# A four-layer graph network on one core: 18 instead of 16 SBUF places for adjacency tiles in layers 0 and 1, and another order of steps in layer 3's loop

## The chip, the cores and the metric

The kernel runs on one core of one Trainium2 chip. The metric is the device time of one execution in microseconds (us), the median of several runs of the same kernel. Engines are named as the profile names them: PE is TensorE (matmuls; PEld its weight loads), DVE is VectorE, ACT is ScalarE, POOL is GpSimd, SP is SyncE, which here only issues DMAs.

## The reference

There are 3327 nodes with 64 features and one dense adjacency matrix `adj` (3327 x 3327 f32, nearly all zeros). Four layers follow one another, with a layernorm and a relu between them, and each reads the whole adjacency:

```python
# layer 0: two gated graph convolutions, each one product with adj
def _ggc(x, adj, W, wih, whh, bih, bhh):
    m = adj @ (x @ W)
    gi = m @ wih.T + bih
    gh = x @ whh.T + bhh
    ...
    r = sigmoid(i_r + h_r); z = sigmoid(i_z + h_z)
    n = tanh(i_n + r * h_n)
    return (1.0 - z) * n + z * x
h = relu(_ggc(x, adj, W1, ...)); relu(_ggc(h, adj, W2, ...))

# layer 1: hyperbolic graph convolution
support_t = mobius_matvec(adj, logmap0(x, c), c)
proj(expmap0(support_t, c), c)

# layer 2: last 100 neighbours, weighted by rank
mask = (adj != 0); rank = cumsum(mask, axis=1)
k = minimum(deg, 100.0)
pos = rank - (deg - k)
w = mask * where(pos > 0, 0.5 ** (k - pos), 0.0)
out = w @ support + bias

# layer 3: attention over pairs of nodes in the Poincare ball
adj_att = sigmoid(left + right.T) * adj
x_local = _logmap(x[:, None, :], x[None, :, :], C)
support_t = einsum('ij,ijd->id', adj_att, x_local)
_proj(_expmap(x, support_t, C), C)
```

## The kernel before

**Blocks, groups and tiles.** The nodes are padded to 26 blocks of 128. The target nodes lie in two groups: g0 with six pairs of blocks, g1 with seven. `gs_` and `gf` are the names of g0 and g1 where side work is written. An adjacency tile is one block of source nodes against one group of targets: (0,k) is 128 x 1536 f32, 768 KB; (1,k) is 128 x 1792 f32, 896 KB. [...]

**The stream of tiles.** Layers 0 to 2 and layer 3 read adjacency tiles in one fixed list of 260 uses. `Stream` keeps them in places ("slots") of SBUF, and loads a tile into a place when it isn't there. The list has these stretches:

| stretch | uses | what it computes |
|---|---|---|
| FIRST | 0 to 25 | first convolution of layer 0, target group 0 |
| SECOND | 26 to 63 | first convolution, group 1 (26 uses); among them, from the tenth, 12 uses of group 0 for the second convolution |
| THIRD | 64 to 103 | the rest of the second convolution |
| LAYER1 | 104 to 155 | layer 1 |
| layer 2 | 156 to 207 | 26 masks of group 1, then 26 of group 0 |
| layer 3 | 208 to 259 | 52 pieces of another width, one for each attention step |

`Stream.done`, called after each use, looks AHEAD 6 uses (10 after SECOND). For each tile there that is missing it evicts the place whose next use is latest, unless that comes sooner than the use it loads for, and issues the load (line 377) on SP's queue. SP does so in order: a load waits for its place to come free, and later loads wait behind it. The number of places is 16 in layers 0, 1 and the first half of layer 2, 7 in its second half, and 4 in layer 3; `Stream.limit` gives it, and a place above the limit of the stretch of its next use counts as free.

**Layers 0 and 1** are one loop: `use` takes the next tile and issues its matmuls `bank<-adj,m_a` or `m_b` (line 620), 1.29 us of PE for a tile of group 0 and 1.504 us for one of group 1. Everything else of these layers (gates, layernorms, the products with weights, the maps of layer 1) is written as generators, the side chains. `weave.tick()` after each use lets each running chain issue its next piece of work; `weave.until` runs a chain out where its result is needed. The side chains of a group's first and second part (`parts_of`) have their own arrays: `big` gives an array of 8 x 64 f32 a partition for each name and part in the pool `w01`, and `gates` has v and e there. `evicted` puts sums into the arrays `m_t0` and `m_t1` of the pool p0.

**Layer 2** makes a mask of each tile (line 1529, VectorE), counts it with matmuls (line 1560), makes weights (line 1572, ScalarE) and multiplies by them (line 1584).

**Layer 3** goes over pairs of blocks in 13 phases: four within group 1 (m = 0 to 3), six between the groups (m = 4 to 9), three within group 0 (m = 10 to 12). `BETWEEN` is 4, `WITHIN` is 10. A phase has two halves b = 0, 1. Its steps and their engines:

| step | engine, line | what |
|---|---|---|
| distances(m,b,i) | PE, 1190 | products of a chunk i of pairs into the one PSUM buffer `pair0` |
| gelus, square | ACT, 1200, 1210 | distances become factors; gelus empties `pair0` |
| tanh_d, tanh_t | ACT, 1223, 1246 | attention, direct and turned pairs |
| attention_d, attention_t | DVE, 1257 | times the adjacency piece; each takes one piece and calls `stream.done` |
| turned(m,k,u) | PE, 1281 | transposes the factors into the PSUM buffer `pair1` |
| factors_d, factors_t | DVE, 1272, 1291 | attention times factors, direct and turned |
| gather_d, gather_t, singles | PE, 1294 | sums over sources |
| end(m) | | drops the phase's arrays; for m = 9 it starts a side chain |

The order in which the steps are issued, and so the order within each engine's queue, is written out by hand in `ORDER3`: a prologue for phase 0, then a loop body that is gone through once for each m from 0 to 14. A word of it is a name, by how many phases the step is late, and the step's arguments: in pass m, `gather_d.2.1` issues gather_d of phase m-2, half 1, and `distances.-1.0.0` that of phase m+1. A step that was issued before, as by the prologue, is left out. `tick.1` always runs the side chains on, `tick.0` only while m is below 4. The side chains of layer 3 are `nodes3(gs_)` at its start, which must be through before phase 4; `finish(gf)` (lines 1372 to 1460), started by `end` of phase 9 in pass 11; and `finish(gs_)` after the loop.

Of the kernel before, what the change touches and what calls it, by code (L numbers as in the profile page):

```python
# [8 lines left out]
F32 = mybir.dt.float32  # L9
# [9 lines left out]
D = 64  # L19
P = 128  # L20
# [22 lines left out]

SLOTS3, SLOTS2, SLOTS01 = 4, 7, 16


AHEAD = (6, 10)
# [23 lines left out]
GROUPS = [Group(0, 6), Group(6, HB)]  # L73
# [91 lines left out]
def places3():  # L165

    r, o = {}, 0
    for m, half, t, w in pieces3():
        r[m, half, t] = (o, w)
        o += w  # L170
    return r, o
# [20 lines left out]
def order3(text):  # L192
# [9 lines left out]
    order3(t)  # L202
    for t in (
        """
        distances.0.0.0 gelus.0.0.0 tanh_t.0.0.0 tick.0 tanh_t.0.0.1 attention_t.0.0 distances.0.0.1
        tick.0 tanh_d.0.0 attention_d.0.0 tick.0 gelus.0.0.1 square.0.0 tick.0 distances.0.1.0 gelus.0.1.0
        tanh_t.0.1.0 tick.0 tanh_t.0.1.1 distances.0.1.1 gelus.0.1.1 tick.0 square.0.1
        turned.0.0.0 tick.0
        """,
        """  # L210
        gather_d.2.1 gelus.0.0.0 attention_t.1.0 distances.0.0.1 tanh_t.0.0.0 factors_t.1.0.0
        tick.0 singles.2.1 end.2 tick.1
        gelus.0.0.1 square.0.0 attention_d.1.0 turned.1.0.1 tick.0 gather_t.1.0.0 distances.0.1.0
        factors_t.1.0.1 factors_d.1.0 tick.1
        tanh_t.0.0.1 gelus.0.1.0 tick.0 tanh_d.0.0 turned.1.1.0 gather_t.1.0.1 gather_d.1.0 attention_t.1.1
        factors_t.1.1.0 tick.1
        distances.0.1.1 singles.1.0 gelus.0.1.1 tick.0 square.0.1 attention_d.1.1 turned.1.1.1
        gather_t.1.1.0 distances.-1.0.0 factors_t.1.1.1 tick.0 factors_d.1.1 tick.1
        turned.0.0.0 tanh_t.0.1.0 tick.0 tanh_d.0.1 tanh_t.0.1.1 gather_t.1.1.1 tick.1
        """,  # L220
    )
]
# [2 lines left out]
class Stream:  # L225
# [16 lines left out]

    def limit(self, t):
        part = sum(t >= s for s in self.starts)
        return (SLOTS01, SLOTS01, SLOTS2, SLOTS3)[part]

    def next_use(self, s, t):

# [44 lines left out]
def gnn_kernel(ctx: ExitStack, tc: tile.TileContext, t, out):  # L293
# [4 lines left out]
    def left(name, **kw):  # L298
        return tc.tile_pool(name=name, bufs=1, side="left", reuse_waits="tile", **kw)

    def right(name, **kw):
        return tc.tile_pool(name=name, bufs=1, side="right", reuse_waits="tile", **kw)
# [6 lines left out]
    p0 = ctx.enter_context(left("p0"))  # L309
    slots_a = ctx.enter_context(left("slots_a"))  # L310
    cc = ctx.enter_context(ExitStack())
    slots_c = cc.enter_context(left("slots_c"))
    c012 = ctx.enter_context(ExitStack())
    slots_b = c012.enter_context(right("slots_b"))
    nd = c012.enter_context(right("nd"))
    c01 = ctx.enter_context(ExitStack())
    w01 = c01.enter_context(right("w01"))
    ps = ctx.enter_context(tc.tile_pool(name="ps", bufs=1, space=PSUM))

# [26 lines left out]
    places, _ = places3()  # L346
# [17 lines left out]

    def load_tile(s, key):
        sum_edges(stream.slots[s][1])
        pool = slots_a if s < SLOTS3 else slots_b if s < SLOTS2 else slots_c
        a = pool.tile([P, WIDE], F32, name="adj", tag=f"adj{s}")
        if len(key) > 2:
            o, w = places[key]  # L370
            src = t["adj3"][:, o : o + w]
        else:
            g, k = key
            w = 2 * GROUPS[g].w
            src = t[f"adj{g}"][k * P : (k + 1) * P, :]
        a = a[:, :w]
        nc.sync.dma_start(a, src)
        loaded[0] += 1
        if loaded[0] in between:
            between[loaded[0]]()  # L380
        return a
# [3 lines left out]
    stream = Stream(load_tile)  # L385
# [68 lines left out]
    def small(g, name):  # L454

        tag = f"s_{name}" if g.part is None else f"s_{name}_{g.part}"
        return p0.tile([P, GROUPS[1].nb], F32, name=name, tag=tag)[:, : g.nb]

    def big(g, name):

        if g.part is None:
            a = p0.tile([P, GROUPS[1].nb, D], F32, name=name, tag="b_" + name)
        else:
            a = w01.tile([P, 8, D], F32, name=name, tag=f"b_{name}_{g.part}")
        return a[:, : g.nb, :]

    def flat(a):
# [229 lines left out]
    for i, (ca, cb) in enumerate(starts):  # L697
        g = Group(ca, cb, part=i % 2)
# [5 lines left out]
    def take_sums(g, acc):  # L704

        for q, (lo, hi) in enumerate(g.chunks):
            cs = slice(g.c0 * P + lo, g.c0 * P + hi)
            V.tensor_copy(mh0[:D, cs], acc[q][:D, : hi - lo])  # L708
            S.activation(hm1[D:, cs], acc[q][D:, : hi - lo], AF.Copy)  # L709

    def gates(g, layer):

        w_mh, w_hm, b, brz = ggc[layer]
        n, cs = g.w, g.cols
        ((p, _, _),) = pieces(1)
        ((p2, _, _),) = pieces(1)
        rz = [p[:, a * 512 : a * 512 + n] for a in range(2)]
        p_h, p_i = (p2[:, a * 512 : a * 512 + n] for a in range(2))

        def product(out, h, w, rs):  # L720
            T.matmul(  # L721
                out[D * (1 - h) : D * (2 - h), :],
                lhsT=w[rs, :],
                rhs=(mh0, hm1)[h][rs, cs],
                start=True,
                stop=True,
            )

        for a in range(2):
            for h in range(2):  # L730
                product(rz[a], h, (w_mh, w_hm)[h][:, a, :], slice(0, P))
        for out, o in ((p_h, 0), (p_i, 1)):
            for h in range(2):
                r = D * ((1 - h) ^ o)
                product(out, h, (w_mh, w_hm)[h][:, 2, :], slice(r, r + D))
        s = []
        for a in range(2):
            s.append(w01.tile([P, 512], F32, name=f"gate{a}", tag=f"gate{a}")[:, :n])
            S.activation(s[a], rz[a], AF.Sigmoid, bias=brz[:, a : a + 1])
        r, z = s  # L740
        v = w01.tile([P, 512], F32, name="v", tag="v")[:, :n]
        V.scalar_tensor_tensor(v, p_h, b[:, 1, 2:3], r, op0=OP.add, op1=OP.mult)
        V.tensor_add(v, v, p_i)
        S.activation(v, v, AF.Tanh, bias=b[:, 0, 2:3])

        e = w01.tile([P, 512], F32, name="e", tag="e")[:, :n]
        V.tensor_sub(e, h_t[:, cs], v)
        V.tensor_mul(e, e, z)
        V.tensor_add(e, e, v)
        V.tensor_scalar(h_t[:, cs], e, 0.0, None, op0=OP.max)  # L750
        if layer == 0:
            S.activation(mh0[D:, cs], e[D:], AF.Relu)
            S.activation(hm1[:D, cs], e[:D], AF.Relu)
        yield 5
# [72 lines left out]
    n = len(s_src) + len(f_src)  # L827
# [10 lines left out]
    n = len(LAYER1) - len(f_src)  # L838
# [88 lines left out]
    gen_f = weave.add(support(gf, acc_f))  # L927
    run(LAYER1[n:], {0: acc_s}, m_a, {}, begun=(0,), ends=(0,))
    c01.close()


    turn["banks"] = (0, 1)
# [570 lines left out]
    def early3():  # L1503

        for name, *args in (("tanh_t", 0, 0), ("tanh_t", 0, 1), ("tanh_d", 0)):
            made3.add((0, name, *args))
            yield from STEPS3[name](0, *args)


    with ExitStack() as c2:  # L1510
# [101 lines left out]
        for n in range(len(work)):  # L1612
            mask(n + 2)
            for part in range(2):
                count(n, part)
                flush(n, 2 if len(todo) > 2 * LAG + 2 else 1)
                todo.append((n, part))
                weave.tick()
            if gen_n or todo[0][0] < NB:
                continue  # L1620

            m_f = evicted(gf, acc2[1], b_l2)
            turn["banks"] = (2, 3)
            c2x.close()
            cc.close()
            stream.close(range(SLOTS2, SLOTS01))
            n3 = ctx.enter_context(left("n3"))
            h = n3.tile([P, NB, D], F32, name="h3")
            c3 = ctx.enter_context(ExitStack())
            n3f = c3.enter_context(left("n3f"))  # L1630
            xd = n3f.tile([P, NB, D], F32, name="xd")

            xs = n3f.tile([P, HN], F32, name="xs")
            xw = n3f.tile([P, HN], F32, name="xw")
            rows_j = n3f.tile([P, NP], BF16, name="rows_j")
            rows_i = n3f.tile([P, NP], BF16, name="rows_i")
            leftb = n3f.tile([P, NP], F32, name="leftb")
            p2c = n3f.tile([P, NB, 31 + ROWS], F32, name="p2c")
            x2, qs, pn, rpn, lefts, righth, B1, Bq2, alq = (
                n3.tile([P, NB], F32, name=n)  # L1640
                for n in "x2 qs pn rpn left righth B1 Bq2 alq".split()
            )
            least = n3.tile([P, 2], F32, name="least")

            packs = [n3f.tile([P, GROUPS[1].nb, P], BF16, name=f"pack{i}") for i in range(2)]
            for a in packs:
                G.memset(a, 0.0)
            G.memset(p2c, 0.0)
            onesl = n3f.tile([12, P], BF16, name="onesl")
            V.tensor_scalar(onesl, last[:12, :].to_broadcast([12, P]), 9.0, None, op0=OP.is_ge)  # L1650
            gen_n = weave.add(nodes3(gf, m_f))
            weave.add(early3(), 1, gen_n)
# [46 lines left out]
    with ExitStack() as cg:  # L1699
# [164 lines left out]
        for o, (g, half) in enumerate(segments):  # L1864
# [6 lines left out]
            for b0 in range(0, g.n, 4):  # L1871
                bs = own[b0 : b0 + 4]
                p = scratch3(b0 // 4)
# [92 lines left out]
            p = scratch3(0)  # L1966
# [101 lines left out]
```

## Time and profile before

| what | value |
|---|---|
| runs | 733.91, 732.25, 730.86 us; median 732.25 |
| the profiled execution's own time | 728.92 us |
| its span in the profile | 727.1 us |
| mean granted PE clock | 0.959 |
| busy: PE, DVE, ACT | 647.2, 463.7, 400.9 us |
| loads of adjacency tiles and pieces | 116 of 896 KB, 92 of 768 KB, 12 of 640 KB |
| use 63, the last of SECOND, on PE | 122.71 to 124.43 us |
| use 155, the last of LAYER1, starts | 292.71 us |
| layer 3's loop | about 430 to 707 us |

A row of the profile's windows gives the length of a stretch, then the busy time of PE, PEld, DVE, ACT and POOL in it with the number of instructions, the granted share of PE's clock, the mean busy share of the core's 16 DMA engines, and GB/s. The page's slice rows have 40 digits, each the busy share of 18.2 us in tenths (9 is 90% or more). The chain of waits follows the work that ended last back from its end; its rows give a start, a length and what the time went to. A row of the waits names the instruction that waited, and behind the arrow what it waited for, then the sum in us, the number of times and the longest.

### The profile page before, as it was taken

What the parts mean: (1) busy time and instruction counts of PE and PEld (TensorE: products, weight loads), DVE (VectorE), ACT (ScalarE), POOL (GpSimd) and SP (SyncE); (2) the same over time, 40 slices, a digit from 0 to 9 for tenths busy, and PEclk for the clock granted to TensorE, in tenths of its full rate; (3) what the DMA queues carried; (4) which work ended last, traced back from release to release, by engine and by line L of the source; (5) the groups of instructions that cost most, each with busy time, mean ns of one, the idle gap of its engine ahead of it and who ended that gap; (6) DMA issues with size and microseconds to landing.
All of it is one profiled execution on the core that took longest, in us unless ns stands there. A gap on an engine that the chain in (4) does not pass through costs nothing.

```text
span 727.1 us, 13405 instructions
## 1 busy us (share of the span) xinstructions
PE 647.2 (89%) x5648; PEld 358.8 (49%) x5648; DVE 463.7 (64%) x758; ACT 400.9 (55%) x577; POOL 6.5 (1%) x11
## 2 busy tenths in 40 slices
PE   3989998999979997889989985899999999998873
PEld 2433442343324332468856652456556666666552
DVE  4314774444778207676576464578888888877884
ACT  3203100302555013788887867688888888885912
POOL 0000000000000000000300000000000000000000
PEclk9999999999999999999999995699999999999995
DMA  8999997599979999999388750146566666553410
GB/s 339 414 415 410 383 357 290 182 405 418 415 270 372 417 415 418 416 368 356 103 290 268 297 159 17 37 138 190 193 199 204 203 204 204 188 175 94 146 49 26
DMA packets 33331, 189.90 MB, mean 261 GB/s; under 512 B 3696, under 2 KB 4848, under 8 KB 33264
## 3 DMA queue, kind: packets, MB, share of 16 engines
q1 hardware_dynamic: 33264, 188.97, 69.7%
q8 instruction: 46, 0.75, 0.4%
q14 instruction: 21, 0.17, 0.1%
HBM read 188.10 MB, written 0.85 MB: 260 GB/s over the span
## 4 chain that ended last, share of the span: by engine, by line
PE 60%; DMA 15%; DVE 13%; ACT 9%; issue 2%; SPq 0%; DVEq 0%; ACTq 0%
PE bank L620 18%; DMA adj<-in_adj 15%; PE bank L1294 13%; PE pair L1190 7%; PE pair L1560 6%; PE bank L1584 5%; PE pair L1281 4%; PE pair L721 2%; ACT tr L1246 2%; DVE dir L1272 2%; DVE dir L1257 1%; ACT w L1572 1%; ACT sq L1200 1%; ACT dir L1223 1%; PE bank L1382 1%
## 5 line engine op out<-in xcount | busy, mean ns | idle before, releaser
L620 PE MATMUL bank<-adj,m_a 128*64 128x384 f32 (+1 forms) x832 | 157.7, 520 | 11.7 <-DMA adj<-in_adj 10.8
L620 PEld LDWEIGHTS bank<-adj,m_a 128*64 128x64 f32 x832 | 56.1, 138 | 103.7 <-issue 65.7
L1572 ACT ACTIVATE w<-pair,ebias 128x896 uint16<-128x896 f32 (+1 forms) x101 | 93.9, 954 | 16.9 <-PE pair L1560 15.6
L620 PE MATMUL bank<-adj,m_b 128*64 128x384 f32 (+1 forms) x416 | 76.7, 515 | 1.4 <-ACT hm L709 1.4
L1529 DVE TENSOR_SCALAR mask<-adj 128x1792 bf16<-128x1792 f32 (+1 forms) x52 | 53.5, 1050 | 24.0 <-PE pair L1560 24.0
L1200 ACT ACTIVATE sq<-pair 128x1024 f32<-128x1024 f32 (+1 forms) x52 | 47.3, 910 | 38.0 <-PE pair L1190 38.0
L1246 ACT ACTIVATE tr<-leftb,righth 128x256 f32<-128x256 f32 x156 | 67.5, 495 | 0.0
L1291 DVE SCALAR_TENSOR_TENSOR tr<-pair,tr 128x1024 f32<-128x1024 f32 (+3 forms) x52 | 50.0, 961 | 26.1 <-PE pair L1281 23.5
L358 DVE SCALAR_TENSOR_TENSOR edges<-adj,edges 128x1792 bf16<-128x1792 f32 (+1 forms) x24 | 45.0, 1890 | 31.1 <-DMA adj<-in_adj 30.9
L1190 PE MATMUL pair<-xs 64*128 64x512 f32 (+3 forms) x120 | 58.0, 570 | 4.8 <-ACT sq L1200 4.7
L1190 PE MATMUL pair<-xs,xw 64*128 64x512 f32 (+3 forms) x120 | 58.0, 570 | 4.7 <-ACT sq L1200 4.7
L1584 PE MATMUL bank<-w,m_b 128*64 128x384 bf16 (+1 forms) x416 | 60.6, 341 | 0.0
L709 ACT ACTIVATE hm<-bank 64x384 f32<-64x384 f32 (+1 forms) x8 | 4.1, 513 | 90.9 <-DVE mh L708 90.8
L1281 PE MATMUL pair<-ident,sq 128*128 128x128 f32 x312 | 47.8, 290 | 7.2 <-DVE tr L1291 3.6
L1257 DVE SCALAR_TENSOR_TENSOR dir<-dir,adj 128x1792 f32<-128x1792 f32 x26 | 52.4, 2016 | 0.0
L1272 DVE SCALAR_TENSOR_TENSOR dir<-sq,dir 128x1792 f32<-128x1792 f32 x26 | 52.4, 2015 | 0.0
L620 PEld LDWEIGHTS bank<-adj,m_b 128*64 128x64 f32 x416 | 29.0, 137 | 45.6 <-issue 42.4
L1223 ACT ACTIVATE dir<-leftb,righth 128x1792 f32<-128x1792 f32 (+6 forms) x38 | 48.4, 1306 | 0.0
L1281 PEld LDWEIGHTS pair<-ident,sq 128*128 128x128 f32 x312 | 35.0, 146 | 26.8 <-issue 13.7
L1210 ACT ACTIVATE sq<-sq,hg 128x1792 f32<-128x1792 f32 x26 | 46.5, 1790 | 0.8
L1294 PE MATMUL bank<-tr,xd 128*64 128x128 f32 x624 | 46.7, 286 | 0.3 <-DVE tr L1291 0.3
L1294 PE MATMUL bank<-dir,xd 128*64 128x384 f32 (+3 forms) x264 | 44.0, 463 | 2.4 <-DVE dir L1272 2.3
(299 smaller groups left out, 998.3 us busy)
## 6 DMA issues: line engine op xcount, KB each, us to landing
adj<-in_adj SPq DMA_DIRECT2D x116, 896.0 KB, 6.9
adj<-in_adj SPq DMA_DIRECT2D x92, 768.0 KB, 9.1
adj<-in_adj SPq DMA_DIRECT2D x12, 640.0 KB, 4.0
xn<-in_x SPq DMA_DIRECT2D x3, 192.0 KB, 5.3
w_l<-in_w_l SPq DMA_DIRECT2D x1, 460.0 KB, 9.8
out<-h_n SPq DMA_DIRECT2D x2, 224.0 KB, 2.3
out<-h_n SPq DMA_DIRECT2D x2, 192.0 KB, 2.4
xn<-in_x SPq DMA_DIRECT2D x1, 256.0 KB, 6.9
```

The lines of the kernel that those rows point to most:

```text
L620: T.matmul(acc[q][h * D : (h + 1) * D, : hi - lo], lhsT=m[:, k, :], rhs=a[:, h * g.w + lo : h * g.w + hi], start=first, stop=last,)
L1190: T.matmul(p[:, o : o + n], lhsT=l, rhs=r, start=not rows, stop=rows)
L1200: S.activation(columns(sqs[m, b], PHASES[m].n)[:, :, lo * P : hi * P], p[:, :, : (hi - lo) * P], AF.Gelu, scale=-HA,)
L1223: S.activation(columns(dirs[m, b], ph.n)[:, :, first * P : first * P + n], left_of(ph.g)[:, :, o : o + n], AF.Tanh, bias=righth[:, 2 * c + ...
L1246: S.activation(a[:, e * 2 * P : (e + 1) * 2 * P].rearrange("p (b c) -> p b c", b=2), left_of(ph.s)[:, :, o : o + P], AF.Tanh, bias=righth[ ...
L1257: V.scalar_tensor_tensor(a[:, :w], a[:, :w], 1.0, stream.tile(stream.now), op0=OP.add, op1=OP.mult)
L1272: V.scalar_tensor_tensor(a, sqs[m, b][:, :n], HD, a, op0=OP.add, op1=OP.mult)
L1281: T.transpose(p[:, o : o + P], columns(sqs[m, b], PHASES[m].n)[:, k, i * P : (i + 1) * P], ident,)
L1294: T.matmul(out, lhsT=lhsT, rhs=rhs, start=False, stop=True, skip_group_check=True)
L1529: V.tensor_scalar(masks[n][:, :w], a, 0.0, None, op0=OP.not_equal)
L1572: S.activation(w, e, AF.Relu, bias=ebias)
L1584: T.matmul(acc2[i][q][h * D : (h + 1) * D, : hi - lo], lhsT=p[:, 2 * c + a, :], rhs=ws[n][:, h * g.w + lo : h * g.w + hi].bitcast(BF16), s ...
```

## The change

It has two parts.

Layers 0 and 1 have 18 places for tiles, layer 2's first half 16 as before: places 16 and 17 lie in a new pool `slots_d` that is closed with layer 1. The room comes from the side chains' arrays. `big` of a part becomes a slice of one array in p0 that both parts share (the second part begins at block 6), and v and e of `gates` lie in `m_t0` and `m_t1`. The instructions of the side chains stay the same.

Layer 3's steps stay the same too, but both texts of `ORDER3` are new. In the loop body, gather_d of the phase before goes from two passes late to one (`gather_d.1.1` for `gather_d.2.1`), and all its gathers stand at the end of the pass behind `turned.0.0.0`; attention_t.0.0 and gelus of the next phase (`gelus.-1.0.0`) stand a pass earlier; tanh_d's second half goes to the head of the next pass. The ticks are 7 of `tick.0` and 5 of `tick.1` for 6 and 5, two of the latter side by side; the prologue has 7 ticks as before.

In the changed kernel the line numbers of layers 0 to 2 are some 6 to 9 higher, those of layer 3's steps by 9 (1190 becomes 1199).

```diff
-SLOTS3, SLOTS2, SLOTS01 = 4, 7, 16
+SLOTS3, SLOTS2, SLOTS1, SLOTS01 = 4, 7, 16, 18
...
-        distances.0.0.0 gelus.0.0.0 tanh_t.0.0.0 tick.0 tanh_t.0.0.1 attention_t.0.0 distances.0.0.1
-        tick.0 tanh_d.0.0 attention_d.0.0 tick.0 gelus.0.0.1 square.0.0 tick.0 distances.0.1.0 gelus.0.1.0
-        tanh_t.0.1.0 tick.0 tanh_t.0.1.1 distances.0.1.1 gelus.0.1.1 tick.0 square.0.1
-        turned.0.0.0 tick.0
+        distances.0.0.0 gelus.0.0.0 distances.0.0.1 tanh_t.0.0.0 attention_t.0.0 tanh_t.0.1.0
+        tanh_t.0.0.1 tick.0 tick.1 tick.0 gelus.0.0.1 distances.0.1.0 square.0.0 gelus.0.1.0
+        attention_d.0.0 tanh_t.0.1.1 distances.0.1.1 tick.0 tick.0 gelus.0.1.1 tick.0 tick.0
+        tanh_d.0.0 square.0.1 turned.0.0.0
         """,
         """
-        gather_d.2.1 gelus.0.0.0 attention_t.1.0 distances.0.0.1 tanh_t.0.0.0 factors_t.1.0.0
-        tick.0 singles.2.1 end.2 tick.1
-        gelus.0.0.1 square.0.0 attention_d.1.0 turned.1.0.1 tick.0 gather_t.1.0.0 distances.0.1.0
-        factors_t.1.0.1 factors_d.1.0 tick.1
-        tanh_t.0.0.1 gelus.0.1.0 tick.0 tanh_d.0.0 turned.1.1.0 gather_t.1.0.1 gather_d.1.0 attention_t.1.1
-        factors_t.1.1.0 tick.1
-        distances.0.1.1 singles.1.0 gelus.0.1.1 tick.0 square.0.1 attention_d.1.1 turned.1.1.1
-        gather_t.1.1.0 distances.-1.0.0 factors_t.1.1.1 tick.0 factors_d.1.1 tick.1
-        turned.0.0.0 tanh_t.0.1.0 tick.0 tanh_d.0.1 tanh_t.0.1.1 gather_t.1.1.1 tick.1
+        tick.1 tanh_d.1.1 factors_t.1.0.0 tick.0 distances.0.0.1 attention_d.1.0 tick.1
+        turned.1.0.1 tanh_t.0.0.0 factors_d.1.0 singles.2.1 gelus.0.0.1 distances.0.1.0 end.2
+        tick.1 square.0.0 factors_t.1.0.1 gather_t.1.0.0 tick.0 turned.1.1.0 gelus.0.1.0
+        tanh_d.0.0 attention_t.1.1 factors_t.1.1.0 tick.1 tick.1 distances.0.1.1 singles.1.0
+        gelus.0.1.1 tick.0 tick.0 square.0.1 attention_d.1.1 tanh_t.0.0.1 tick.0 turned.1.1.1
+        tanh_t.0.1.0 tick.0 distances.-1.0.0 factors_t.1.1.1 factors_d.1.1 tick.0 gelus.-1.0.0
+        turned.0.0.0 gather_t.1.0.1 gather_t.1.1.0 attention_t.0.0 gather_d.1.0 tanh_t.0.1.1
+        gather_t.1.1.1 gather_d.1.1
...
     def limit(self, t):
         part = sum(t >= s for s in self.starts)
-        return (SLOTS01, SLOTS01, SLOTS2, SLOTS3)[part]
+        return (SLOTS01, SLOTS1, SLOTS2, SLOTS3)[part]
...
     c01 = ctx.enter_context(ExitStack())
+    slots_d = c01.enter_context(right("slots_d"))
     w01 = c01.enter_context(right("w01"))
...
-        pool = slots_a if s < SLOTS3 else slots_b if s < SLOTS2 else slots_c
+        limits = ((SLOTS3, slots_a), (SLOTS2, slots_b), (SLOTS1, slots_c), (SLOTS01, slots_d))
+        pool = next(p for most, p in limits if s < most)
...
+    bigs = {}
+
     def big(g, name):
 
         if g.part is None:
             a = p0.tile([P, GROUPS[1].nb, D], F32, name=name, tag="b_" + name)
         else:
-            a = w01.tile([P, 8, D], F32, name=name, tag=f"b_{name}_{g.part}")
+
+            if name not in bigs:
+                bigs[name] = p0.tile([P, GROUPS[1].nb, D], F32, name=name, tag="b_" + name)
+            a = bigs[name][:, 6 * g.part :, :]
         return a[:, : g.nb, :]
...
+    spares = [p0.tile([P, GROUPS[1].w], F32, name="m_t", tag=f"m_t{i}") for i in range(2)]
+
     def gates(g, layer):
...
-        v = w01.tile([P, 512], F32, name="v", tag="v")[:, :n]
+        v, e = (a[:, :n] for a in spares)
...
-        e = w01.tile([P, 512], F32, name="e", tag="e")[:, :n]
...
     c01.close()
+    stream.close(range(SLOTS1, SLOTS01))
...
-            stream.close(range(SLOTS2, SLOTS01))
+            stream.close(range(SLOTS2, SLOTS1))
```

## The prediction

> **What bounds the kernel now.** I read the page's engine line and slices first, then the chain of waits in order of time, then windows of the stretches that the change touches, then the waits of layer 3's end.
>
> ```profile
> span 727.1 us, 13405 instructions
> PE 647.2 (89%) x5648; PEld 358.8 (49%) x5648; DVE 463.7 (64%) x758; ACT 400.9 (55%) x577; POOL 6.5 (1%) x11
> ...
> PE   3989998999979997889989985899999999998873
> ...
> DMA  8999997599979999999388750146566666553410
> ...
> PE 60%; DMA 15%; DVE 13%; ACT 9%; issue 2%; SPq 0%; DVEq 0%; ACTq 0%
> ```
>
> TensorE is busy nearly everywhere, so only a stretch where its digit falls can shorten, unless its work shrinks; and this change leaves the work as it is. Such stretches are few: the start, about slices 15 to 17 (LAYER1), slice 24 (entry of layer 3), and the last four. DMA ends 15% of the chain. Where? These four waits in a row are the largest (start in us, length, what):
>
> ```profile
> 227.84 16.36 DMA adj<-in_adj
> 244.21 17.52 DMA adj<-in_adj
> 261.76 15.77 DMA adj<-in_adj
> 277.59 15.07 DMA adj<-in_adj
> ```
>
> The windows (length, then busy time of PE, PEld, DVE, ACT, POOL, granted clock, DMA share, GB/s) say the same:
>
> ```profile
> 16.00:62.00 46.00, 41.57 (x240) 17.08 (x240) 11.85 (x41) 5.83 (x12) 0.00 (x0) 1.00 1.02 415
> 84.00:116.00 32.00, 32.00 (x186) 13.11 (x184) 21.45 (x12) 0.00 (x0) 0.00 (x0) 1.00 0.97 365
> 125.00:196.00 71.00, 70.18 (x411) 27.50 (x411) 36.59 (x64) 18.29 (x34) 0.00 (x0) 1.00 0.86 341
> 228.00:295.00 67.00, 61.13 (x329) 21.96 (x326) 27.29 (x98) 14.35 (x25) 0.00 (x0) 1.00 1.02 417
> ```
>
> A DMA share of 1.0 with idle PE is a stretch bound by loads: 16 to 62 (FIRST, where every tile is new) and the end of LAYER1, where from 259.6 to 292.7 each use starts 0.04 us after its tile lands. SECOND's last four uses (118.3 to 122.7) are like that too. The other two windows have a full PE: a load saved there is worth nothing by itself. For layer 3:
>
> ```profile
> 430.60:450.00 19.40, 11.26 (x39) 4.59 (x38) 10.26 (x18) 13.64 (x18) 0.00 (x0) 0.61 0.27 82
> 450.00:470.00 20.00, 13.25 (x80) 8.17 (x81) 12.20 (x35) 10.57 (x17) 0.00 (x0) 0.61 0.03 4
> 470.00:490.00 20.00, 18.90 (x226) 12.01 (x226) 15.36 (x20) 17.63 (x25) 0.00 (x0) 1.00 0.48 153
> ...
> 550.00:590.00 40.00, 39.98 (x454) 25.00 (x454) 35.32 (x22) 35.34 (x51) 0.00 (x0) 1.00 0.61 202
> 590.00:630.00 40.00, 39.97 (x482) 25.27 (x482) 35.21 (x23) 35.30 (x52) 0.00 (x0) 1.00 0.62 200
> ...
> 670.00:690.00 20.00, 15.71 (x164) 9.56 (x162) 16.91 (x26) 19.88 (x38) 0.00 (x0) 0.91 0.43 124
> ```
>
> From 550 to 650 PE is never idle (0.05 us in 100): a phase takes 18.3 us, a half 9.15, which is the sum of PE's steps in a half: distances 1.28 + 1.02, singles 1.66, turned 0.80 + 1.02, gather_t 1.02 + 0.71, gather_d 1.65. VectorE and ScalarE are busy 0.88 of it. An order of steps can't shorten that. PE's idle time lies at the entry (14.9 us from 430.6 to 470), in the within phases (2.9 from 470 to 550) and in the tail (9.4 from 650 to 706.8). The waits of the tail (us in total, times, longest):
>
> ```profile
> ACT sq L1200 <- PE pair L1190: 6.0, 1, 6.0
> PE pair L1190 <- ACT sq L1200: 5.8, 3, 2.5
> DVE f_e L1405 <- PE bank L1382: 5.2, 1, 5.2
> DVE f_nn L1452 <- ACT f_nn L1445: 2.6, 1, 2.6
> ```
>
> These are finish(gf), woven into the last phases. Its VectorE step waits 5.2 us for a matmul of its own (L1382) that stands in PE's queue behind distances (L1190), which wait for gelus (L1200) to empty pair0. VectorE is idle 5.22 us there, 1.82 at 663 and 2.64 at 673: 9.7 in all; then it is full from 676 to 705.
>
> [...] the 5.2 us above is a whole VectorE queue behind one step. [...] 0.61 granted from 430 to 470 and 1.00 where PE is full[...]. [...] the trace moves 415 to 417, 2.19 us for 896 KB and 1.89 for 768.
>
> **Part 1: 18 places.** I followed the stream's rule (evict what is used latest, look AHEAD 6 or 10 uses) over all 260 uses. Layers 0 and 1 need 120 tile loads for 128, 101.6 MB for 108.7: 7.1 MB, 17 us at 415 GB/s. By stretch: FIRST 31 and 31, SECOND 23 and 21, THIRD 34 and 32, LAYER1 40 and 36. What each is worth:
> - FIRST: 0, no tile comes twice.
> - SECOND: tiles (0,10) and (0,11) stay. The last uses are then PE's: use 60 starts at 116.33, three more at 1.505 put use 63 at 120.85, not 122.71: **−1.9**.
> - THIRD: 0. PE is idle 0.8 us of 71; DMA runs further ahead but the entry of LAYER1 waits for a side chain.
> - LAYER1: (1,15) and (1,16) are not loaded again, 2 × 2.19 = 4.4; with two places more one load fits ahead of the entry of layer 1, 2.2 sooner. Its last tile lands 4.4 + 2.2 = 6.6 sooner, at 286 for 292.7. PE alone would be there at 283, so the loads still decide: **−6.5** (5.5 to 7.5).
> - Layer 2: its first half loads 23 for 21, its second 23 for 22, as the places are closed before it. Cost 0: every tile landed at least 8.2 us before its mask (L1529); the loads that come anew have 10 us. Without that cover each costs 2.2.
> - The arrays put inside others: the parts' big arrays become slices of one, the gates' v and e lie in m_t0 and m_t1. No instruction more or less; the side chains' waits on VectorE, ScalarE and PE are the same in the two builds. Cost 0; layer 2's masks that lie over the new places start after use 154, no later than now.
>
> Sum **−8.4** (6 to 10).
>
> **Part 2: the loop of layer 3.** The same instructions, in another order. Every queue is concerned: on SP, the loads follow attention_t.0.0, which comes a pass sooner, so its piece's successor is asked for sooner; pieces have about 0.6 of the DMA, so 0 for that.
> - Steady phases, 550 to 650: 0, if PE stays full. What covers PE changes: see the slower rival.
> - Within phases: 2.9 us of PE idle, mostly L1190 waiting for L1200 (2.0). gelus.0.0.0 now stands at the end of the pass before, right after its distances, before the tick: **−2**.
> - Tail: the 5.22 goes down to about 1, since gelus come ahead of the tick and pair0 is free when finish(gf)'s matmul is queued; two ticks side by side hand VectorE the next step without a phase's step in between. The 2.64 (ScalarE's root behind a table load, 1.28) stays, of the 1.82 some. 9.7 to about 5, and as VectorE is full afterwards this passes to the end: **−4.5**. What is late next: VectorE itself, factors_d and attention at 2.02 each; the last 20.5 us, finish(gs), are as before.
> - Entry, 430.6 to 470: 12 ticks a pass for 11, as many in the prologue, distances.0.0.1 earlier. PE and ScalarE are both waiting there for nodes3(gs), a chain. No row shows the new order: bounded by −3 and +3, I take 0.
>
> Sum **−6.5**, from −11 to +4.
>
> **The number.** −8.4 − 6.5 = −14.9 on the profiled execution's 728.9 (span 727.1 + 1.8): 714.0. The median of the runs is 3.3 above that execution, 732.25, so **717.3**.
>
> **Rivals.**
> - The loop gives nothing, or costs a little (wait moves from L1405 to another step of the chain, the tail stays at 9.7 idle): 732.25 − 8.4 = 723.9, with +3 at the entry 727. For: ScalarE and VectorE at 0.88 leave little room. Against: the tail's wait has one nameable cause.
> - The loads saved don't pay: PE or the side chain support(gf), which ends near 284, is right behind, or the DMA falls idle elsewhere. Then −1 to −3 for part 1, and 722 to 725. For: 17 us of DMA give only 8.4 already. Against: DMA share 1.02 for 67 us.
> - **Slower**: pair0 is one buffer. distances.0.1.0 now comes straight after gelus.0.0.1; before, turned (1.02) and gather_t (1.02) lay between on PE. Now PE has turned 1.02 and singles 1.66 between the two distances, 2.7 us, while ScalarE must do tanh_t (four at 0.495, 2.0) and gelus (0.8), 2.8, and may still have tanh_d (1.78) before them. If PE stalls there in each half, some 20 halves pay: from 0.42 us a half the 8.4 are eaten, from 0.6 the kernel is over 0.5% slower, at 0.8 it is 16 − 8.4 = +7.6, **740**. Against: ScalarE has 1.2 us spare in each half, so it can be early.
> - The change doesn't do what it says: the slices serialise the two parts' side chains, and layer 1's entry slips. The build has the same waits, so I give it 1 in 100, in the slower case.
>
> **How the numbers follow.** Both parts pay, 712 to 721: 0.50. Loop for nothing or a small loss, 721 to 728: 0.23. Loads for little: 0.09. Ends even: 0.09. Slower: 0.09. A measurement of this kernel tells about 0.5% from no change, 3.7 us, so faster means under 728.6: 0.50 + 0.23 + 0.09 = 0.82 (a few of these cases end above, a few even ones below). Same 0.09, slower 0.09. The range, 707 to 729, leaves out the slower case, half of the even one and a gain beyond −25 (0.05); the likeliest case's own is 712 to 721.
>
> **What would show it.** Right: the page's adj issues fall from 220 (116 + 92 + 12) to 215; use 63 starts 1.9 us sooner, the last use of LAYER1 8.4; windows of the middle phases still 18.3 us a phase with PE full; the wait of L1405 below 2 us. Wrong: PE idle before L1190 (there L1199) in every half; mask waits on DMA in layer 2; an unchanged idle sum of VectorE in the tail.

## The result and the profile after

The changed kernel is faster: 711.72 us median (708.52 to 713.05, 4 runs) beside 732.03 us of the kernel before (730.86 to 733.91), a ratio of 0.971 (95% interval 0.967 to 0.976). The profiled execution took 713.05 us with a span of 711.2, which is 15.9 less than the span before. The medians are 20.3 apart, so both profiles together understate the gain by some 4 us; what follows accounts for the 15.9.

The page's head, the slices of PE and DMA, the chain by engine, and the loads of tiles:

```profile
span 711.2 us, 13400 instructions
...
PE 640.8 (90%) x5648; PEld 362.6 (51%) x5648; DVE 463.2 (65%) x758; ACT 401.5 (56%) x577; POOL 5.9 (1%) x11
...
PE   3988999999979998889998994699999999999692
...
DMA  8999996599959999978687942046666666654400
...
PE 67%; DMA 13%; DVE 9%; ACT 8%; issue 2%; SPq 1%; DVEq 0%; ACTq 0%
...
adj<-in_adj SPq DMA_DIRECT2D x110, 896.0 KB, 5.8
adj<-in_adj SPq DMA_DIRECT2D x93, 768.0 KB, 8.2
```

There are 215 loads (110 + 93 + 12), as forecast. PE's busy time fell by 6.4 us for the same 5648 matmuls, which the forecast had excluded. Waits for DMA at the end of LAYER1 in the chain (start, length):

```profile
237.83 16.91 DMA adj<-in_adj
254.76 16.52 DMA adj<-in_adj
271.36 15.06 DMA adj<-in_adj
```

Three rows where there were four, but still there: LAYER1 ends on its loads. The windows of layer 3 (length, busy time of PE, PEld, DVE, ACT, POOL, granted clock, DMA share, GB/s):

```profile
426.00:446.00 20.00, 9.29 (x50) 4.79 (x46) 14.25 (x28) 14.69 (x20) 0.00 (x0) 0.79 0.25 79
446.00:466.00 20.00, 14.98 (x84) 9.61 (x84) 8.73 (x25) 11.71 (x17) 0.00 (x0) 0.61 0.12 34
466.00:486.00 20.00, 19.54 (x250) 12.81 (x252) 17.49 (x22) 17.39 (x25) 0.00 (x0) 1.00 0.50 158
...
538.00:578.00 40.00, 40.00 (x470) 26.24 (x470) 35.93 (x23) 36.33 (x54) 0.00 (x0) 1.00 0.64 209
578.00:618.00 40.00, 40.00 (x458) 25.27 (x456) 35.95 (x24) 36.32 (x52) 0.00 (x0) 1.00 0.62 201
...
654.00:674.00 20.00, 14.06 (x155) 8.35 (x152) 17.88 (x38) 18.36 (x34) 0.00 (x0) 0.98 0.52 159
```

PE is full in the middle in both kernels, yet a phase takes 17.92 us where it took 18.30. The waits of the tail, from 630 to 691 us (total, times, longest):

```profile
DVE tr L1300 <- PE pair L1290: 5.0, 3, 1.9
ACT sq L1209 <- PE pair L1199: 4.5, 3, 2.5
...
PE pair L1290 <- ACT sq L1219: 2.8, 1, 2.8
DVE f_e L1414 <- PE bank L1391: 2.2, 1, 2.2
...
PE pair L1199 <- ACT sq L1209: 1.6, 1, 1.6
```

finish(gf)'s wait for its own matmul fell from 5.2 to 2.2 us, and its wait for ScalarE's root (2.6) is gone. VectorE's waits for turned (L1290) have grown to 5.0 us in three pieces; in the kernel before, from 645 to 707 us, they were

```profile
DVE tr L1291 <- PE pair L1281: 2.1, 2, 1.8
```

With landmarks that exist in both traces, the 15.9 us can be split. A landmark is the start of an instruction; fd(m,b) is factors_d of phase m, half b. Intervals in us:

| stretch | before | after | difference | forecast |
|---|---|---|---|---|
| start to use 63, last of SECOND | 122.7 | 120.7 | −2.0 | −1.9 |
| to use 155, last of LAYER1 | 170.0 | 165.7 | −4.3 | −6.5 |
| to the last product of layer 2 | 137.6 | 139.8 | +2.2 | 0 |
| to fd(0,1): entry of layer 3 | 46.3 | 44.2 | −2.1 | 0 |
| to fd(4,1): within phases | 73.1 | 68.6 | −4.5 | −2 |
| to fd(9,1): middle phases | 91.5 | 89.6 | −1.9 | 0 |
| to fd(12,1): tail | 61.9 | 59.3 | −2.6 | −4.5 |
| to the end | 24.0 | 23.3 | −0.7 | 0 |

The sum was forecast within 1 us (−14.9 for −15.9), out of terms that are wrong on both sides: that it came so near is luck. The experiments go after these terms.

### The profile page after: what moved, and what is told of

It is laid out like the page before. It is cut to its first block, busy times and chain, and to the rows that moved or that the text cites. A ratio compares the mean times of both kernels' runs of the same rounds, so it can differ in the third digit from the quotient of the medians.

```text
span 711.2 us, 13400 instructions
## 1 busy us (share of the span) xinstructions
PE 640.8 (90%) x5648; PEld 362.6 (51%) x5648; DVE 463.2 (65%) x758; ACT 401.5 (56%) x577; POOL 5.9 (1%) x11
## 4 chain that ended last, share of the span: by engine, by line
PE 67%; DMA 13%; DVE 9%; ACT 8%; issue 2%; SPq 1%; DVEq 0%; ACTq 0%
PE bank L626 21%; PE bank L1303 15%; DMA adj<-in_adj 12%; PE pair L1199 7%; PE pair L1569 6%; PE pair L1290 6%; PE bank L1593 5%; PE pair L730 2%; ACT w L1581 1%; DVE dir L1266 1%; DVE mask L1538 1%; PE bank L1391 1%; PE pair L531 1%; DVE dir L1281 1%; ACT sq L1219 1%
## 5 line engine op out<-in xcount | busy, mean ns | idle before, releaser
L1199 PE MATMUL pair<-xs,xw 64*128 64x512 f32 (+3 forms) x120 | 56.3, 555 | 5.4 <-ACT sq L1209 5.4
L1199 PE MATMUL pair<-xs 64*128 64x512 f32 (+3 forms) x120 | 56.3, 555 | 1.2 <-ACT sq L1209 1.2
L1290 PE MATMUL pair<-ident,sq 128*128 128x128 f32 x312 | 47.7, 290 | 10.7 <-ACT sq L1219 9.1
L1290 PEld LDWEIGHTS pair<-ident,sq 128*128 128x128 f32 x312 | 34.7, 145 | 29.3 <-ACT sq L1219 9.5
L1266 DVE SCALAR_TENSOR_TENSOR tr<-tr,adj 128x1280 f32<-128x1280 f32 (+2 forms) x26 | 45.5, 1750 | 1.6 <-ACT tr L1255 1.6
L1303 PE MATMUL bank<-dir,p2c 128*32 128x256 f32 (+1 forms) x440 | 45.3, 350 | 0.0
```

The source lines that it names most:

```text
L1199: T.matmul(p[:, o : o + n], lhsT=l, rhs=r, start=not rows, stop=rows)
L1266: V.scalar_tensor_tensor(a[:, :w], a[:, :w], 1.0, stream.tile(stream.now), op0=OP.add, op1=OP.mult)
L1290: T.transpose(p[:, o : o + P], columns(sqs[m, b], PHASES[m].n)[:, k, i * P : (i + 1) * P], ident,)
L1303: T.matmul(out, lhsT=lhsT, rhs=rhs, start=False, stop=True, skip_group_check=True)
```

## Experiments

Ratios are to the kernel before, with their 95% intervals; kernels without a ratio were run once, and are read by the intervals of the table. Two of these hardly depend on the run: 68.58 to 68.60 within phases and 89.63 or 89.64 in the middle, wherever nothing there was changed. The entry and the tail do depend on it, and so does the time that PE spends there at half its clock (granted 0.50): the same tail takes 61.9 us in the kernel before, 6.8 of them at half clock, and 65.1 in layout_only below, 13.7 of them at half clock.

### The two parts alone, and the shared memory alone

places_only is the changed kernel with the old texts of `ORDER3`; loop_only is the kernel before with the new ones; layout_only is places_only with

```diff
-SLOTS3, SLOTS2, SLOTS1, SLOTS01 = 4, 7, 16, 18
+SLOTS3, SLOTS2, SLOTS1, SLOTS01 = 4, 7, 16, 16
```

> 18 places in layers 0 and 1, layer 3's order as in the kernel before. Theory: the two parts add up, and this one brings what the traces show up to the last use of LAYER1: use 63 starts 2.0 us sooner, use 155 6.3 us sooner, layer 3's loop as long as before (430 to 707), so 6 us less, ratio about 0.991, 215 loads. Rival: the gain is lost again behind, in layer 2 or at the entry of layer 3, which waits for chains of its own: less than 3 us, ratio above 0.996. Second rival: the order of the loop hides part of the places' gain, then this run shows more than 8 us.

> 16 places, layer 3's loop in the new order. Theory: 12 us less, ratio about 0.983, made of 2 at the entry, 3 to 4 in the within phases, 2 in the middle phases (17.92 us a phase for 18.30), 3 to 4 in the tail; use 155 starts at 292.7 as before. Rival: the sum was owed to the earlier start of layer 3 [...], then 5 to 8 us.

> The arrays lie within others' memory as in the changed kernel, but layers 0 and 1 have 16 places, and layer 3's order is that of before: what the sharing of memory costs by itself. Theory: nothing, within 1 us of before, use 155 at 292.7. Rival: the parts' side chains wait for one another, and a stretch of layers 0 and 1 is 1 to 4 us longer, at most at the entry of layer 1 (use 104 later than 205.8).

places_only: 724.64 us, ratio 0.992 (0.990 to 0.995). loop_only: 718.82, ratio 0.984 (0.980 to 0.987). Their product is 0.976, beside 0.971 and 0.974 (0.971 to 0.978) for both together in two comparisons: the parts add up. In us, places_only is 6.3 faster than the kernel before and loop_only 12.1, where the forecast had 8.4 and 6.5: the loop brought nearly twice its share, the places less than theirs. layout_only: ratio 1.0001 (0.9986 to 1.0015): putting arrays inside others costs nothing that its 20 runs show.

In the one trace of layout_only use 155 started at 294.2, later than in the two others with 16 places (292.7 and 293.2), but 0.7 to 0.9 us of that stand already at use 63, which the traces with 18 places also have spread over 1.4 us (120.6 to 122.0; in places_only 122.0, so 0.7 sooner than before and not 2.0). With 18 places and the stream unchanged the eight traces at hand have use 155 from 284.7 to 287.2, 286.2 in the mean, so the places bring 7.1 us there on average, 2.0 of them by use 63, and the 6.3 of the first pair of traces is on the low side.

### The changed kernel again: what layer 2 lost

> The changed kernel once more, for its trace. Theory: the 2.1 us that its first trace lost in layer 2 (the lead fell from 6.3 to 4.1 us at 315) were a window of 3.4 us in which PE had half its clock after a pause, and such windows fall by chance: in this trace the lead at the end of layer 2 is 6 us or the window lies elsewhere, and the time goes with the number of such windows, some 1.7 us each at most. Rival: the loss is of the changed load plan, and stands in the same place with PE at full clock.

It took 712.00 us. Its layer 2 took 138.0 us, not 139.8, so the loss isn't part of the load plan. The windows of the first trace after, and of the same work before, show what it was:

```profile
314.00:318.00 4.00, 3.15 (x18) 1.90 (x19) 3.17 (x4) 2.70 (x3) 0.00 (x0) 0.61 0.56 182
```

```profile
318.00:322.00 4.00, 2.67 (x28) 1.83 (x29) 2.40 (x5) 3.83 (x6) 0.00 (x0) 1.00 0.90 360
```

In the upper row (after) PE is busy 3.15 us of 4 with 18 matmuls, in the lower (before) 2.67 us with 28: the granted clock is at half (0.50) for 3.4 us, from 314.9, and the lead over the kernel before falls from 5.9 to 4.2 us across it. This half-clock window follows pauses of PE of 1.0 and 1.1 us; the kernel before has the same two pauses there, and a clock of 1.00 behind them. What makes such a window isn't shown. Counted over the traces of the study, layer 2 takes 136.6 and 136.9 us without such a window (layout_only, ticks_apart), 137.5 to 138.4 with one (seven traces; ahead_at_entry below, whose first mask waits, is left out), 138.7 to 139.8 with two (four traces). After had two, before one.

### The places: 17, and a longer look ahead

places_17 has 17 for 18 in the first line above. ahead_at_entry is the changed kernel with

```diff
         most = AHEAD[self.now >= len(FIRST + SECOND)]
+        if 96 <= self.now <= 112:
+            most = 14
```

and ahead_16 has `102 <= self.now <= 120` and 16.

> The changed kernel with 17 places in place of 18. By the stream's rule layers 0 and 1 load 124 tiles (120 with 18, 128 with 16), and LAYER1 38 (36, 40). Theory: the gain of LAYER1 goes with its loads, one place is worth half: use 155 starts 2 to 3 us later than with 18, at 289 to 290, and use 63 within 0.5 us of it. Rival: the second place brings nothing more, since DMA falls idle at the entry of layer 1 for as long as a load is saved: 286 to 287.

> The changed kernel, but the stream looks 14 uses ahead from use 96 to 112, not 10. Theory: in the changed kernel DMA falls idle for 13 us around the entry of layer 1 (202 to 241 us) since all of the next 10 tiles are there; four more uses let three or so loads of LAYER1 go in that gap, so that the last tile lands 3 to 5 us sooner and use 155 starts at 282 to 284 for 286.5; layers 2 and 3 as they are: 3 to 4 us less than the changed kernel, ratio to before about 0.969. Rival: places, not the look ahead, hold the loads back, or the side chain support(gf) ends last: less than 1 us.

> The changed kernel, but the stream looks 16 uses ahead from use 102 to 120, not 10. In the run with 14 (96 to 112) use 155 started 3.4 to 4.1 us sooner than in the changed kernel, and most of it was lost as layer 2's first mask waited 2.9 us for tile (1,24), which that plan had evicted and loaded last. This plan keeps (1,24) to (1,21) in places that layer 2 can use. Theory: use 155 starts at 282 to 284, the first masks don't wait for DMA, and the lead of 3 to 4 us lasts to the end: ratio to before 0.967 to 0.970. Rival: another wait takes its place at the start of layer 2 (the side chain support(gf), or the masks' memory over places 16 and 17), and less than 1.5 us of it is left.

With 17 places use 155 started at 290.3: somewhat under half of the gain of 7.1, about as the loads of LAYER1 go (38, between 36 and 40). Its use 63 was at 122.1, 1.4 later than in the trace after, where at most 0.5 had been expected.

Why did the places bring 4 us in LAYER1 (5.1 in the mean of the traces), and not 6.5? The stream's rule, followed over the uses, asks for the same ten tiles of LAYER1 ahead of use 104 in both kernels; what the places save are two later loads, (1,15) and (1,16), the 4.4 us of the forecast. The other 2.2 were to come from one more load ahead of the entry, but a look of ten uses ahead doesn't ask for one.

In the trace after, all ten have landed at 202.54, before use 104 starts (203.40); in the kernel before three of them land after it (205.75). Then the stream is silent until 204.95: all of the next ten tiles are in their places while the entry of layer 1 waits for a side chain. The windows of that stretch, after and before:

```profile
202.00:241.00 39.00, 36.96 (x214) 14.74 (x214) 31.79 (x144) 16.33 (x31) 0.00 (x0) 0.95 0.79 294
```

```profile
202.00:241.00 39.00, 35.26 (x206) 13.63 (x204) 32.55 (x142) 18.23 (x33) 0.00 (x0) 0.96 0.83 328
```

In the upper row the DMA moves 294 GB/s, where from 16 to 62 us in the kernel before, at a share of 1.02, it moves 415; no packet at all is under way in 5.3 of these 39 us. Counted by landings, with 2.19 and 1.89 us for a tile of 896 and 768 KB, more is lost: 13.0 us in six pieces from 202 to 241 in the kernel after, 8.9 from 202 to 244 in the one before. So much of what fewer loads had freed was idled away before LAYER1's last loads began.

ahead_at_entry fills part of that (7.0 us are lost from 200 to 241): use 155 started at 283.1, 3.4 us sooner than in the first trace after and 4.1 than in the second. But the kernel gained nothing (711.47, ratio 0.973, 0.968 to 0.978). The mask's tile in its trace (from 278 to 292 us, the start of layer 2; what VectorE idled for before masks, and how long):

```profile
  DMA adj<-in_adj: 2.9, 1
```

The first mask's tile (1,24) had been in a place that layer 2 doesn't have; it was loaded once more, behind LAYER1's last tile, and landed at 285.24; the mask starts at 285.36. Of a lead of 4.1 us over the trace of after_again 1.0 was left at the first count. ahead_16 keeps that tile (2.1 us are lost): use 155 started at 283.0, no mask waits for DMA, and the time is 707.69 us (705.89 to 708.26), ratio 0.969 (0.966 to 0.972). That is the version which beats both kernels; its interval overlaps that of the changed kernel, but its four runs lie below all eight of that kernel (708.52 to 713.05), and its trace shows 3 to 4 us at the end of LAYER1 that last.

### The loop: prologue, gelus, ticks, gathers, end

Five runs of the changed kernel with one thing, or one group of words, put back. Once each, they took 714.7 (old_prologue), 711.3 (gelus_late), 711.6 (ticks_apart), 716.4 (gathers_apart) and 719.4 us (end_early). old_prologue has the old first text of `ORDER3`. The others, in the loop body (read by the landmarks of the table above):

```diff
 gelus_late
-        tick.1 tanh_d.1.1 ...     (and ... tick.0 gelus.-1.0.0 at the end)
+        tick.1 gelus.0.0.0 tanh_d.1.1 ...
 ticks_apart
-        ... factors_t.1.1.0 tick.1 tick.1 ... factors_d.1.1 tick.0 gelus.-1.0.0
+        ... factors_t.1.1.0 tick.1 ... factors_d.1.1 tick.0 tick.1 gelus.-1.0.0
 gathers_apart
-        ... distances.0.0.1 attention_d.1.0 ... turned.0.0.0 gather_t.1.0.1 gather_t.1.1.0 attention_t.0.0 gather_d.1.0
+        ... distances.0.0.1 gather_d.2.0 attention_d.1.0 ... gather_t.1.0.1 turned.0.0.0 gather_t.1.1.0 attention_t.0.0
 end_early
-        ... distances.0.0.1 attention_d.1.0 tick.1 ... singles.2.1 gelus.0.0.1 distances.0.1.0 end.2 tick.1
+        ... distances.0.0.1 singles.2.1 end.2 tick.1 attention_d.1.0 ... gelus.0.0.1 distances.0.1.0 tick.1
```

> The changed kernel with the prologue's text of before and the new loop body. Between the last product of layer 2 and factors_d(0,1) the changed kernel takes 44.1 us, the kernel before 46.2. Theory: the prologue brings that, as it lets the side chain nodes3(gs) run on two to three steps sooner: 46 us again, and the rest as in the changed kernel. Rival: the loop's first pass brings it (one tick more, and the order of its ticks): 44 us stay.

The entry took 48.0 us for 44.2, more than the 46.3 of the kernel before. A landmark between, fd(0,0), tells why (us):

| prologue, loop body | last product of layer 2 to fd(0,0) | fd(0,0) to fd(0,1) |
|---|---|---|
| old, old (before) | 34.5 | 11.8 |
| new, new (after) | 29.9 | 14.2 |
| old, new (old_prologue) | 34.3 | 13.8 |

The new prologue brings 4.3 to 4.5 us up to fd(0,0), and the new body loses some 2 us of that again in the rest of the entry: the −2.1 of the table is what is left. The first column is steady: 34.5 to 35.4 in three traces with both texts old, 29.9 in nine of ten with both new (31.3 in ticks_apart). The second is less so, 11.4 to 12.1 and 11.5 to 14.2, so the size of that loss is uncertain; PE is at half its clock for 20.5 to 37.5 us around the entry, most in old_prologue.

> The changed kernel, but gelus.0.0.0 stands behind the first tick of the pass, as in the kernel before, in place of gelus.-1.0.0 at the end of the pass before. Theory: this step made the tail's gain, since it empties pair0 before finish(gf) queues matmuls behind it: the wait of f_e for PE grows from 2.2 to 4 us or more, factors_d(9,1) to (12,1) takes 61.9 us as before for 59.3, and the within phases, (0,1) to (4,1), take 1 to 2 us more than 68.6. Rival: the gain of the tail comes from the pair of ticks and the placing of gathers; then both intervals stay within 0.5 us.

Nothing moved: within phases 68.60, tail 59.31, and the same wait:

```profile
DVE f_e L1414 <- PE bank L1391: 2.2, 1, 2.2
```

gelus.-1.0.0 brought none of the gain. Its tail even had three half-clock windows of PE, where old_prologue and ahead_16, with the changed loop, take 60.6 and 60.5 us with three; whether the old place is the better one a single run doesn't tell.

> The changed kernel with the gathers of a phase taken apart again: gather_t.1.0.1 ahead of turned.0.0.0, gather_d.1.0 in the next pass behind distances.0.0.1 (as gather_d.2.0). Theory: a PE step takes longer where the step before it was of another kind; the new order has gathers side by side, which makes a middle phase 17.92 us for 18.30, so this one is at 18.1 to 18.3 with PE full. Rival: the 0.38 us come from elsewhere (shorter distances, fewer short idle times not shown), and 17.92 stays.

The middle phases went to 18.2 us each (91.1 for 89.6 over five), with PE as full as ever:

```profile
540.00:580.00 40.00, 40.00 (x464) 25.22 (x462) 35.37 (x23) 35.48 (x50) 0.00 (x0) 1.00 0.61 193
```

So 0.3 of the 0.38 us that a phase lost lie in which steps stand side by side on PE. (gather_t.1.0.0 keeps its place in the middle of the pass in all of these orders; the other gathers stand at its end in the changed kernel.) In the trace before, gather_t's 12 matmuls between turned and gather_d take 0.71 us and gather_d ahead of distances 1.60 to 1.69, from the start of a step to the start of the next. In the trace after, a run of 28 gather_t matmuls takes 1.58, where 16 and 12 apart took 1.02 + 0.71, the other 12 take 0.66 between two gather_d, and a gather_d between gathers takes 1.50. Over a phase that is 0.20 us in gather_t and 0.18 in gather_d, which is all of the 0.38. Its within phases took 69.6 for 68.6, about 0.24 a phase. Its end took 3.2 us more: gather_d of phase 12's first half now stands behind that of the second half, which waits for factors_d(12,1), so the last gather_d ends 7.1 us after that landmark, not 3.9.

> The changed kernel, but the second of the two ticks side by side stands behind factors_d.1.1 and its tick, where the kernel before had its last but one. Theory: the pair lets finish(gf) go on in one go, so that VectorE issues a chain of short operations without a wait between (the wait of f_nn for ScalarE, 2.6 us before, was gone): apart, a wait of 1 us or more stands in finish(gf) again, and factors_d(9,1) to (12,1) takes 1 to 2.5 us more than 59.25. Rival: the tail's gain comes from the gathers' places and PE's shorter steps: 59.25 within 0.5.

No wait of f_nn came back, and f_e waits 2.2 us as in the changed kernel. The tail took 61.1 us, but with four half-clock windows of PE in it; places_17 and ahead_at_entry, whose loop is that of the changed kernel, took 61.3 with as many, while the trace after had two. So the pair of ticks isn't the cause either.

> The changed kernel, but singles.2.1, end.2 and the tick behind it stand right after distances.0.0.1, as in the kernel before; so finish(gf) starts ahead of the pass's second distances, and between the two distances PE has turned (1.02 us) beside what stays, not turned and singles. Theory: the place of end.2 makes the tail's gain: the wait of f_e for PE, 5.2 us before and 2.2 in the changed kernel, is over 4 again, and VectorE's idle time from factors_d(9,1) to (12,1), 11.7 us before and 9.6 in the changed kernel, is 11 or more. Rival: it comes from the rest of the order, and both stay. For pair0: with less cover on PE a middle phase takes over 17.92 us, up to 18.6, if the forecast's slower case has substance; if ScalarE is early enough it stays 17.92 within 0.1.

Here the tail moves, by far more than expected: it took 67.9 us for 59.3, and its waits are

```profile
DVE f_e L1414 <- PE bank L1391: 12.1, 1, 12.1
...
PE pair L1199 <- ACT sq L1209: 7.1, 3, 4.1
...
ACT sq L1368 <- PE bank L1303: 5.1, 1, 5.1
```

finish(gf) is started by `end.2`. Started ahead of the second distances of the pass, its VectorE step is queued in front of that phase's factors_t and attention_t, while its matmul lies behind distances that wait for gelus. The three rows are one chain, read from below: finish(gf)'s first ScalarE step waits 5.1 us for PE's sums, the gelu behind it in ScalarE's queue comes late, PE's distances wait up to 4.1 us for that gelu, and finish(gf)'s matmul (L1391) stands behind these distances, so that its VectorE step waits 12.1. VectorE is idle 17.9 us of the tail (67.9 less 50.0 busy), beside 9.6 in the changed kernel and 11.7 in the one before. Half-clock windows may have a part in the 8.6 us, five (17.0 us) for two (6.8); PE is idle 9.1 us in this tail, 5.9 in the changed kernel's. So in the new order the tail hangs on where `end.2` stands, with singles.2.1 and the tick that move along with it; how much of the 2.6 us between the kernels is due to its move alone isn't settled, since the old order with a later `end.2` wasn't run. And the middle phases: 17.92 us, as in the changed kernel, although PE has only turned between the pass's first two distances.

## Why the prediction was right or wrong

The measured 711.7 lies in the range (707 to 729) and the change is a clear gain, as the likeliest case had it; the number itself, 717.3, is 5.6 high. About 1 us of that is the sum (714.0 forecast for the profiled execution, 713.05 measured). The rest is the step from a profiled execution to a median: the forecast kept the 3.3 us by which the runs before lay above their profile, while the runs after lie 1.3 below theirs. That the sum fits is luck: the runs of the parts alone give −6.3 for the places (−8.4 forecast) and −12.1 for the loop (−6.5), and of the loop's gain some 4 us are shorter PE steps, which the forecast had ruled out.

- **FIRST, SECOND, THIRD: right.** Use 63 started 2.0 us sooner for 1.9 (2.0 in the mean of the traces too); (0,10) and (0,11) had been waiting in their places for 83 us. 16 to 62 us is bound by loads as before (DMA share 1.02 and 415 GB/s in both).
- **LAYER1: mis-sized.** "With two places more one load fits ahead of the entry of layer 1, 2.2 sooner" failed. The last tile landed at 286.42, near the 286 forecast, but that number had been worked out without the 2 us by which everything then ran ahead: the loads gained 4.3 us relative to SECOND (5.1 in the mean), about the two loads that LAYER1 no longer repeats. The number of loads ahead of the entry stayed at ten, since it is set by the look of ten uses ahead and not by the places; the rest went into DMA's idle time at the entry. ahead_16, which looks further, gains 8.5 us over the kernel before in this stretch.
- **Layer 2: right in the mean.** Mask waits for loads didn't come. Of the 2.2 us lost in the first trace 1.7 went in one half-clock window of 3.4 us; after_again lost 0.4.
- **The shared arrays: right.** layout_only, ratio 1.0001.
- **Entry: the value taken, 0, was wrong, within its bounds.** −2.1, of which the prologue brings −4.3 to −4.5 and the loop body costs some 2.
- **Within phases: the idle time was right, the rest missing.** PE's idle time there fell from 2.9 to 0.5 us. The other 2.2 us are PE's busy time becoming shorter; gathers_apart gives 1.1 of it back, the rest isn't traced to a word of the order. That gelus would do it was wrong: gelus_late has the same time.
- **Middle phases: "an order of steps can't shorten that" was wrong.** I had added up PE's steps with the durations that they have in the old order; these durations differ with the steps next to them (gather_t's 12 matmuls take 0.71 us between turned and gather_d, 0.66 between two gather_d). 0.38 us a phase, gathers_apart gives 0.3 of it back.
- **Tail: sign right, size and cause wrong.** L1405 fell to 2.24, not to 1; L1452's 2.64 didn't stay but vanished; the waits for turned grew from 3.1 to 5.3 between the landmarks. VectorE's idle time went from 11.7 to 9.6 us by the landmarks. Neither gelus ahead of the tick nor the pair of ticks, which I had named, has a part in it. The place of end.2, which I had not listed, can move the tail by more than the whole gain; its share of the 2.6 stays open.
- **The slower rival: refuted.** pair0 has cover enough: the middle phases stayed at 17.92 even with singles moved away from between the two distances. ScalarE is early, as the argument against it said: in these phases of end_early it waits 8.7 us for distances.
- **The rival of loads that don't pay** has a true core: 7.1 MB less are 17 us of DMA at 415 GB/s, and some 6 of them reach the clock (places_only).

## What to carry to other kernels

A load plan that needs fewer loads brings its bound forward only as far as the stream asks for the next ones in time: look in the trace for idle DMA ahead of the stretch that waits for loads. The place at which a side chain begins in the main loop can matter more than the order of the loop's own steps: in end_early the side chain's VectorE step waited 12.1 us for a matmul that stood behind others in PE's queue, and the tail was 8.6 us longer. And when PE is full, a new order of the same steps can still be worth something: here a phase fell from 18.30 to 17.92 us, 2%, as its gathers took 0.38 us less.

## What the runs showed of the hardware

- PE's granted clock fell to 0.50 for stretches of 3.4 us or multiples of it: in the traces before and after 3.4, 6.8, 17.1 and 23.9 us, and a last one, of 16.0 and 14.0 us, that was still on at the end of the span. What draws one isn't shown: in the trace after, one began behind two pauses of 1.0 and 1.1 us with 1.4 us of work between them, and in the kernel before the clock stayed at 1.00 behind the same two pauses. What I had not expected is their weight in an already busy kernel. In layer 2 the traces took some 1 to 1.7 us more for each. The tail of layer 3 takes 59.2 or 59.3 us with two (after, after_again, loop_only, gathers_apart), 59.3 to 60.6 with three (gelus_late, old_prologue, ahead_16) and 61.1 to 61.3 with four (ticks_apart, places_17, ahead_at_entry); in the old order, 61.9 with two (before, places_only) and 65.1 with four (layout_only). Runs of one kernel differ by 1.1 us (loop_only) to 6.0 (layout_only); how much of that is windows isn't shown.
- PE, shown as busy 100% in 540 to 580 us in gathers_apart and in 538 to 578 in the kernel after, did a phase in 18.2 and in 17.9 us. The busy share didn't tell the two apart.
- A load that waited for its place held up SP's queue: at the entry of layer 3 in the kernel before, one waited 35.7 us for attention_t (L1257), and SP issued no load from 433.0 us until 468.8.
